# Two pacing constants of the last image's depthwise convolution are lowered, so its taps are laid out denser on VectorE

## The chip, the cores and the metric

The kernel runs on one core of a Trainium2 chip. The metric is the device time of one execution in microseconds. All arithmetic is float32. The engines are named as in the profile: PE is TensorE, DVE is VectorE, ACT is ScalarE, POOL is GpSimd, SP is SyncE, which issues most DMAs.

## The reference

The input is x, 8 images of 384 channels by 32 by 32. Two layers follow one another.

Layer 0 is a transformer block over the 1024 pixels of an image: layernorm, q, k and v, eight heads of attention, a projection with a residual, layernorm, and an MLP with a residual.

```python
xn = layernorm(xf, g1, beta1)
qkv = jnp.einsum('bnc,oc->bno', xn, w_qkv) + b_qkv
...
x1 = out + shortcut
xn2 = layernorm(x1, g2, beta2)
h = jax.nn.gelu(jnp.einsum('bnc,oc->bno', xn2, w_fc1) + b_fc1, approximate=False)
y = x1 + jnp.einsum('bnh,oh->bno', h, w_fc2) + b_fc2
```

Layer 1 takes that result and computes a depthwise convolution of 7 by 7, a layernorm over channels, w1 with GELU, a global response normalization (GRN), and w2 with a residual.

```python
y = jax.lax.conv_general_dilated(x, dw_w, padding=((3, 3), (3, 3)), feature_group_count=DIM, ...)
y = (y - mu) * jax.lax.rsqrt(var + EPS) * ln_w + ln_b
y = jax.nn.gelu(jnp.einsum('bhwc,cd->bhwd', y, w1) + b1, approximate=False)
gx = jnp.sqrt(jnp.sum(jnp.square(y), axis=(1, 2), keepdims=True))
nx = gx / (jnp.mean(gx, axis=-1, keepdims=True) + GRN_EPS)
y = grn_gamma * (y * nx) + grn_beta + y
return identity + (jnp.einsum('bhwd,dc->bhwc', y, w2) + b2)
```

## The kernel before

**Layout and stages.** Channels lie on the 128 partitions in three tiles (ct = 0, 1, 2), pixels along the free axis, in halves of 512. An iteration of the loop in `main` (L1543) does the attention and the MLP of image b and the second layer of image b-1. The depthwise convolution is no matrix product: it is 49 multiply-adds (taps) per channel tile on DVE (`convolution`, L972; L996 for the first tap, L998 for the others), spread beside PE's products. The convolution of image b runs on DVE while PE works on w1 and w2 of image b-1 and on the attention and the MLP of image b+1.

**The last image.** Image 7 has no later image beside which its convolution could run. So its MLP is done by halves of the pixels (`mlp_by_halves`, L928): fc1 and fc2 of half 0, then of half 1. A convolution row needs three rows on either side, so rows 0 to 12 can be convolved once half 0 is through, and rows 13 to 31 after half 1. As each of fc2's three output tiles is done, DVE adds it to the residual (`add_first`, L794), ACT copies it into the padded image (`pad_half`, L790), and `last_convolution` (L1530) is called. On the first tile of each half it starts a convolution: 147 taps (3 x 49) over 13 rows, then 147 over 19 rows. The second is hung behind the first.

Three layernorms follow in the same way, over the rows in `LAST` (L1138): norm a (rows 0 to 12, 416 pixels) is hung behind the first convolution, norm b (rows 13 to 21, 288 pixels) behind the second, norm c (rows 22 to 31, 320 pixels) behind norm b. Each is a chain over four engines (`layernorm`, L399): two adds on DVE (L413, L416), a sum over channels as a product with ones on PE (ln_sum, L380), the subtraction of the mean on DVE (L423), squares on ACT (L430), two adds on DVE (L434, L437), a second sum on PE (ln_var, L380), logarithm and exponential on ACT (L447, L448), and the scaling on DVE (L451).

PE meanwhile does, in this order: fc2 of half 0, fc1 and fc2 of half 1 (L351), w1 of image 6 (`grn_up_straight`, L1091, products at L338), w1 of image 7 for rows 0 to 12 (`last_up`, L1160, products at L1168, tiles h_last; it needs norm a), five of the six blocks of w2 of image 6 (`grn_down_straight`, L1104, products at L1124, added to the residual on DVE at L1132), w1 of image 7 for rows 13 to 21 (needs norm b) and for rows 22 to 31 (needs norm c), the last block of w2 of image 6, and w2 of image 7. Image 6's own layernorm (a chain of the same lines, with its channel sums folded by two DMAs on POOL, L388 and L394) runs during fc2 of half 0 and fc1 of half 1. The GRN scale of image 6 (`grn_scale`, L1176) starts as the first h_last tiles do: a product over gx (gxsum, L1182), a chain of small DVE operations (L1185 to L1190), and the scaling of w2's first tiles on DVE (L1210) and ACT (L1207).

**What sets the order.** All engines run programs that are written in one pass; each engine executes its own in order. `Flow` (L112) keeps a clock, `now`, that counts the planned length of PE's products (0.857 us for one of 512 columns, L67). A chain is a Python generator that yields how long to wait until its next step. After every product, the chains that are due write their next instructions. A chain started with `paced=True` counts its waits from when the last step was due, the others from when it was written. `finish` writes all that is left of a chain at once. `after` (L1230) lets a chain begin when another one has been written to its end, asking every 1.0 us.

In `convolution` the mean planned distance of two taps is `us`; each tap's own share of it goes by its size (L980). So 147 taps take 147 x `us` of planned time, whatever DVE needs for them. A step that is written early is not executed early unless its engine is free; it stands ahead of what is written after it.

**Buffers around it.** PSUM has four single banks, tag "o" (fc1, fc2, norm sums, gxsum, h_last, w2), and two pairs, tag "s" (w1 of image 6). A bank is given again when its last reader is done. Weights are held in a ring of nine tiles (`Weights`, L254), loaded by SP in the order of use. SP also stores the image (`keep`, L953), which waits for the last L794.

Of the kernel before, what the change touches and what calls it, by code (L numbers as in the profile page):

```python
# [151 lines left out]
def block_kernel(  # L152
# [71 lines left out]
    def col(name, i):  # L224
        at, width = VEC[name]
        assert i < width
        return vec[:, at + i : at + i + 1]

    def inner(ct):
        return pad[:, ct, PAD : PAD + H, PAD : PAD + W]  # L230

    def image(ap):
        return ap.rearrange("p (h w) -> p h w", h=H)
# [729 lines left out]
    def inside(dy, dx, y0, y1):  # L963

        rows = slice(max(y0, PAD - dy), min(y1, H + PAD - dy))
        return rows, slice(max(0, PAD - dx), min(W, W + PAD - dx))

    def size(dy, dx, y0, y1):
        rows, cols = inside(dy, dx, y0, y1)
        return 120 + (rows.stop - rows.start) * (cols.stop - cols.start)  # L970

    def convolution(acc, us, first=(), y0=0, y1=H, ready=tuple(range(CT)), taken=None):  # L972

        done = [0] * CT
        ct, n = None, 0
        taps = KS * KS - (HELPED if taken is not None else 0)

        shares = [size(*divmod(i, KS), y0, y1) for i in TAPS[:taps]]  # L980
        shares = [taps * s / sum(shares) for s in shares]
        while min(done) < taps:
            left = [c for c in ready if done[c] < taps and not (taken and taken.get(c, 0) > flow.now)]
            if not left:
                yield 1.0
                continue
            ct = min([c for c in left if c != ct] or left, key=lambda c: done[c])
            i = done[ct]
            share = shares[i]
            dy, dx = divmod(TAPS[i], KS)  # L990
            rows, cols = inside(dy, dx, y0, y1)
            window = inner(ct)[:, rows.start + dy - PAD : rows.stop + dy - PAD, cols.start + dx - PAD : cols.stop + dx - PAD]
            dst = image(acc[:, ct, :])[:, rows, cols]
            tap = col("dww", ct * KS * KS + TAPS[i])
            if i == 0:
                nc.vector.tensor_scalar(dst, window, tap, col("dwb", ct), ALU.mult, ALU.add)  # L996
            else:
                nc.vector.scalar_tensor_tensor(dst, window, tap, dst, ALU.mult, ALU.add)  # L998
            done[ct] += 1
            n += 1  # L1000
            yield share * next((early for m, early in first if n <= m), us)
# [228 lines left out]
    def after(first, chain, us=0):  # L1230
        if us:
            yield us
        while first is not None and first.gi_frame is not None:
            yield 1.0
        yield from chain
# [202 lines left out]
    def main():  # L1438
# [52 lines left out]
        def conv_norm(b, ln):  # L1491

            if b > 0:
                acc = state["acc"]
                how = dict(wait=5.0) if b < B - 1 else dict(wait=3.4, factor=2.4)
                norm = abreast(acc, acc, eps1, "lnw", f"ln3_{b - 1}", True, **how)
                if b < B - 1:
                    norm = sequence(norm, block_differences(acc))
                state["norm3"] = flow.spawn(after(ln, after(state["help"], after(state["conv"], norm))))

        def next_norms(b):

            if b > 0:
                flow.finish(state["help"])
                flow.finish(state["conv"])
            if b + 1 < B:
                xn = state["xn"] = load_x(b + 1, "xn")
                name = f"ln1_{b + 1}"
                places = (lambda: weight_places(name)) if b else averages
                norm = abreast(xn, xn, eps0, "g1", name, True, places=places, gentle=b > 0, factor=1.4 if b else 1.7)  # L1510
                state["norm1"] = flow.spawn(after(state["norm3"], norm, 50 if b else 11))
# [11 lines left out]
        last = wqkv[:, : CT * N].rearrange("p (c n) -> p c n", c=CT)  # L1523

        def last_norm(part, slow):
            return layernorm(last, last, part, eps1, "lnw", f"ln3_{B - 1}", True, slow=slow)

        ready = [], []

        def last_convolution(h, ct, ln=None):  # L1530
            if ct < 0:
                conv_norm(B - 1, ln)
                next_norms(B - 1)
                return
            ready[h].append(ct)
            if ct == 0:
                rows = (LAST[0].stop // W, H) if h else (0, LAST[0].stop // W)
                conv = convolution(last, 0.86 if h else 0.66, (), *rows, ready[h])
                state["conv"] = flow.spawn(after(state["conv"], conv), paced=True)
                if h == 0:  # L1540
                    state["norm_a"] = flow.spawn(after(state["conv"], last_norm(LAST[0], 2.6)))

        for b in range(B):  # L1543
# [6 lines left out]
            if b < B - 1:  # L1550
                mlp(b, xt, xn, weights, b, ln2, rest, lambda: next_norms(b), lambda ln: conv_norm(b, ln))
            else:
                acc = state["acc"]
                mlp_by_halves(b, xt, xn, weights, ln2, rest, last_convolution)
# [184 lines left out]
```

## Time and profile before

| what | us |
|---|---|
| median of six runs | 3304.83 (3301.5 to 3305.07) |
| the profiled execution, its own time | 3301.38 |
| its span | 3299.6 |
| PE busy | 3269.9 (99%) |
| DVE busy | 2396.8 (73%) |
| first convolution on DVE (first and last start of the stretch) | 2947.8 to 3040.3 |
| second convolution on DVE | 3040.3 to 3167.4 |
| norm a: ln_sum and ln_var on PE | 3050.62 and 3066.77 |
| gxsum of image 6 on PE; L1190 on DVE | 3098.49; 3099.57 |
| norm b: from L413 to the first h_last behind it | 3169.07 to 3176.21 |
| w2 of image 6, first five blocks on PE | 3116.86 to 3168.38 |

Lines of the profile give an engine, a line of the kernel, the operation, the tiles (written <- read), shapes, a count, busy time, and the idle time before with what ended it. A float32 product counts as two records on PE. The granted clock is 1.00 when TensorE runs at full speed. The waits view has the engine and line that waited, what it waited for, the total, the times, and the longest.

### The profile page before, as it was taken

What the parts mean: (1) busy time and instruction counts of PE and PEld (TensorE: products, weight loads), DVE (VectorE), ACT (ScalarE), POOL (GpSimd) and SP (SyncE); (2) the same over time, 40 slices, a digit from 0 to 9 for tenths busy, and PEclk for the clock granted to TensorE, in tenths of its full rate; (3) what the DMA queues carried; (4) which work ended last, traced back from release to release, by engine and by line L of the source; (5) the groups of instructions that cost most, each with busy time, mean ns of one, the idle gap of its engine ahead of it and who ended that gap; (6) DMA issues with size and microseconds to landing.
All of it is one profiled execution on the core that took longest, in us unless ns stands there. A gap on an engine that the chain in (4) does not pass through costs nothing.

```text
span 3299.6 us, 38767 instructions
## 1 busy us (share of the span) xinstructions
PE 3269.9 (99%) x14296; PEld 1408.2 (43%) x14296; DVE 2396.8 (73%) x3186; ACT 1605.5 (49%) x2194; POOL 484.3 (15%) x569
## 2 busy tenths in 40 slices
PE   8999999999999999999999999999999999999998
PEld 4344434443344433444344443444434444344455
DVE  4445787887857978579786797767876788879840
ACT  2542663446634375353662636526474355623541
POOL 2121210112110121101211021110221112100000
PEclk9999999999999999999999999999999999999999
DMA  5336732657245563537436374273842647333231
GB/s 198 112 108 147 151 67 69 159 116 151 56 99 140 137 126 57 130 109 167 92 58 144 103 184 76 53 167 90 186 72 60 179 90 173 70 78 90 68 97 43
DMA packets 199109, 368.73 MB, mean 112 GB/s; under 512 B 40768, under 2 KB 46784, under 8 KB 198528
## 3 DMA queue, kind: packets, MB, share of 16 engines
q0 software_dynamic: 80896, 158.63, 26.3%
q1 hardware_dynamic: 117728, 206.83, 20.8%
q8 instruction: 115, 1.88, 0.2%
q10 hardware_dynamic: 288, 0.71, 0.1%
q14 instruction: 82, 0.67, 0.1%
HBM read 187.03 MB, written 34.60 MB: 67 GB/s over the span
## 4 chain that ended last, share of the span: by engine, by line
PE 89%; DMA 0%; issue 0%; DVE 0%; POOL 0%; ACT 0%; POOLq 0%; DVEq 0%
PE fc L351 15%; PE s L664 11%; PE o L684 11%; PE h L358 10%; PE fc_p L358 10%; PE o_p L358 9%; PE qk L358 6%; PE o L1124 4%; PE proj L606 3%; PE v L592 3%; PE h_last L1168 2%; PE h L338 2%; PE ln_var L394 1%; PE ln_sum L394 0%; PE ln_var L380 0%
## 5 line engine op out<-in xcount | busy, mean ns | idle before, releaser
L998 DVE SCALAR_TENSOR_TENSOR acc<-pad,vec,acc 128x870 f32<-128x870 f32 (+7 forms) x861 | 963.9, 1156 | 9.0 <-DMA acc<-tap 4.3
L673 ACT ACTIVATE p<-s 128x1024 f32<-128x1024 f32 x512 | 524.3, 1024 | 282.8 <-PE s L664 275.7
L664 PE MATMUL s<-qk 48*64 48x512 f32 x4096 | 546.7, 592 | 0.2 <-ACT qk L505 0.2
L684 PE MATMUL o<-p,v 64*64 64x512 f32 x4096 | 543.2, 589 | 0.0
L351 PE MATMUL fc<-xn,fc 128*128 128x512 f32 x1152 | 502.3, 594 | 0.0
L1020 POOL DMA_DIRECT2D acc<-tap x294 | 253.5, 876 | 1209.1 <-ACT tap L1019 776.4
L351 PEld LDWEIGHTS fc<-xn,fc 128*128 128x128 f32 x1152 | 217.5, 190 | 280.6 <-issue 269.0
L358 PE MATMUL fc_p<-hid,fc 128*128 128x512 f32 x728 | 317.7, 593 | 0.0
L370 ACT ACTIVATE hid<-fc,bfc_f 128x512 f32<-128x512 f32 x192 | 131.3, 686 | 344.0 <-PE fc L351 343.8
L684 PEld LDWEIGHTS o<-p,v 64*64 64x64 f32 x4096 | 163.3, 133 | 280.7 <-issue 272.3
L664 PEld LDWEIGHTS s<-qk 48*64 48x64 f32 x4096 | 159.7, 133 | 279.2 <-issue 223.2
L358 PE MATMUL o_p<-y,w 128*128 128x512 f32 x624 | 270.9, 592 | 0.0
L1069 DVE TENSOR_TENSOR y<-h,y 128x512 f32<-128x512 f32 x288 | 197.0, 690 | 89.8 <-PE h L358 75.2
L1019 ACT ACTIVATE tap<-pad,vec 128x512 f32<-128x512 f32 x294 | 213.0, 734 | 19.5 <-DMA acc<-tap 19.4
L358 PEld LDWEIGHTS fc_p<-hid,fc 128*128 128x128 f32 x728 | 137.7, 190 | 176.4 <-issue 172.4
L358 PE MATMUL h<-acc,w_A 128*128 128x512 f32 x432 | 207.3, 595 | 0.0
L358 PEld LDWEIGHTS o_p<-y,w 128*128 128x128 f32 x624 | 118.0, 190 | 148.7 <-issue 132.0
L998 DVE SCALAR_TENSOR_TENSOR wqkv<-pad,vec,wqkv 128x377 f32<-128x377 f32 (+24 forms) x288 | 177.4, 694 | 0.6
L625 DVE TENSOR_TENSOR attn<-o,attn 128x512 f32<-128x512 f32 x64 | 44.2, 690 | 166.6 <-ACT attn L623 166.6
L790 ACT COPY pad<-x 128x512 f32<-128x512 f32 x48 | 30.2, 635 | 248.4 <-DVE x L856 192.5
L549 DVE TENSOR_TENSOR qk<-qk,qk 128x512 f32<-128x512 f32 x168 | 114.5, 689 | 37.2 <-PE qk L358 28.2
L592 PE MATMUL v<-wqkv,xn 128*128 128x384 f32 x384 | 127.7, 490 | 0.0
(311 smaller groups left out, 3750.7 us busy)
## 6 DMA issues: line engine op xcount, KB each, us to landing
acc<-tap POOLq DMA_DIRECT2D x294, 256.0 KB, 3.5
w_A<-in_w SPq DMA_DIRECT2D x72, 384.0 KB
fc<-s_fc SPq DMA_DIRECT2D x91, 256.0 KB
hid<-hid POOLq DMA_DIRECT2D x42, 512.0 KB, 7.1
fc<-in_wfc SPq DMA_DIRECT2D x54, 384.0 KB
w<-s_w SPq DMA_DIRECT2D x78, 256.0 KB
y<-y POOLq DMA_DIRECT2D x36, 512.0 KB, 7.0
kept<-x SPq DMA_DIRECT2D x8, 1536.0 KB
```

Source lines behind the costliest of these rows:

```text
L351: nc.tensor.matmul(out=ps, lhsT=lhsT(k), rhs=rhs(k)[:, half(h)], start=(k == 0), stop=(k == nk - 1))
L358: nc.tensor.matmul(out=bank, lhsT=lhsT, rhs=rhs, start=k == 0, stop=k == len(pairs) - 1)
L370: nc.scalar.activation(dst, src, function, **kw)
L592: nc.tensor.matmul(out=ps[:, :C], lhsT=xn[:, k, t * P : (t + 1) * P], rhs=wv_sb[:, k, :], start=(k == 0), stop=(k == CT - 1),)
L664: nc.tensor.matmul(out=s[64 * i : 64 * i + 64, j, :], lhsT=kT[64 * j : 64 * j + HD, m, k0 : k0 + 64], rhs=qT[64 * j : 64 * j + HD, m, half ...
L673: nc.scalar.activation(p, s, AF.Exp)
L684: nc.tensor.matmul(out=outs[i][64 * j : 64 * j + 64, :], lhsT=v[keys, t, at : at + 64], rhs=p[keys, j, :], start=(t == 0), stop=(t == KT - 1),
L998: nc.vector.scalar_tensor_tensor(dst, window, tap, dst, ALU.mult, ALU.add)
L1019: nc.scalar.mul(t.rearrange("p (h w) -> p h w", w=W), window, tap)
L1020: nc.gpsimd.dma_start(out=acc[:, ct, half(h)], in_=t, accum_op=ALU.add)
L1069: nc.vector.tensor_tensor(dst, bank, part, ALU.add)
L1124: nc.tensor.matmul(out=ps, lhsT=tiles[k], rhs=y(k, part), start=(k == 0), stop=(k == HT - 1))
```

## The change

The two paces of the last image's convolution are lowered: from 0.66 to 0.56 us per tap for the first 13 rows, and from 0.86 to 0.72 for the other 19. The taps, their order among themselves and all other instructions are the same. In the written order, 147 taps take 82.3 us of planned time instead of 97.0, and then 105.8 instead of 126.4. What is hung behind a convolution is written earlier by as much, and more taps stand ahead of what is written at a fixed point beside them.

```diff
             if ct == 0:
                 rows = (LAST[0].stop // W, H) if h else (0, LAST[0].stop // W)
-                conv = convolution(last, 0.86 if h else 0.66, (), *rows, ready[h])
+                conv = convolution(last, 0.72 if h else 0.56, (), *rows, ready[h])
                 state["conv"] = flow.spawn(after(state["conv"], conv), paced=True)
                 if h == 0:
                     state["norm_a"] = flow.spawn(after(state["conv"], last_norm(LAST[0], 2.6)))
```

## The prediction

> **What bounds the kernel now.** Read first: the busy shares and the chain that ended last. TensorE is busy for 99% of the span, and the chain runs on it.
>
> ```profile
> span 3299.6 us, 38767 instructions
> PE 3269.9 (99%) x14296; PEld 1408.2 (43%) x14296; DVE 2396.8 (73%) x3186; ACT 1605.5 (49%) x2194; POOL 484.3 (15%) x569
> PE 89%; DMA 0%; issue 0%; DVE 0%; POOL 0%; ACT 0%; POOLq 0%; DVEq 0%
> ```
>
> So time is gained or lost only where TensorE waits. Second: the waits of TensorE between 2940 and 3180 us, the stretch in which the last image's convolution lies.
>
> ```profile
> PE ln_var L380 <- DVE ln_sq L437: 2.4, 1, 2.4
> PE ln_sum L380 <- DVE ln_a L416: 1.7, 1, 1.7
> PE h_last L1168 <- DVE wqkv L451: 1.6, 1, 1.6
> ```
>
> All three belong to the second layernorm (rows 13 to 21, "norm b"), which starts only when the convolution is through, after 3168 us. They sum to 5.7 us. Behind them the clock is lower, by the windows (length, PE, PEld, DVE, ACT, POOL, granted clock, DMA):
>
> ```profile
> 3172.00:3174.00 2.00, 0.74 (x2) 0.50 (x2) 0.96 (x3) 1.80 (x3) 0.00 (x0) 0.56 0.00 1
> 3176.00:3178.00 2.00, 1.79 (x4) 1.36 (x5) 1.91 (x5) 0.90 (x1) 0.00 (x0) 0.50 0.00 0
> 3180.00:3184.00 4.00, 4.00 (x18) 3.11 (x17) 1.29 (x3) 2.62 (x9) 0.00 (x0) 1.00 0.34 98
> ```
>
> Third: what VectorE has free in the same stretch.
>
> ```profile
> 2947.00:3041.00 94.00, 91.26 (x170) 1.00 0.34 93
> 3041.00:3095.00 54.00, 52.15 (x75) 1.00 0.14 38
> 3099.00:3168.00 69.00, 60.58 (x91) 1.00 0.32 92
> ```
>
> This view carries the forecast: over the first convolution (2947 to 3041) VectorE is busy 91.26 of 94 us. Fourth: the timeline of VectorE, for the places where another engine needs it (start, length, line, operation).
>
> ```profile
> 2977.81 0.69 DVE L437 TENSOR_TENSOR attn<-attn 128x512 f32<-128x512 f32 x1
> 3029.60 0.75 DVE L794 SCALAR_TENSOR_TENSOR x<-fc,vec,x 128x512 f32<-128x512 f32 x1
> 3042.59 0.59 DVE L416 TENSOR_TENSOR ln_a<-ln_a,wqkv 128x416 f32<-128x416 f32 x1
> 3060.76 0.59 DVE L437 TENSOR_TENSOR ln_sq<-ln_sq,ln_sq 128x416 f32<-128x416 f32 x1
> 3075.26 18.88 DVE L998 SCALAR_TENSOR_TENSOR wqkv<-pad,vec,wqkv 128x551 f32<-128x551 f32 x26
> 3098.65 0.17 DVE L1185 TENSOR_REDUCE gmean<-gxsum 128x1 f32<-128x12 f32 x1 [4.51 <-PE gxsum L1182]
> 3099.57 0.17 DVE L1190 TENSOR_SCALAR gscale<-gscale 128x12 f32<-128x12 f32 x1
> 3100.66 22.82 DVE L998 SCALAR_TENSOR_TENSOR wqkv<-pad,vec,wqkv 128x589 f32<-128x589 f32 x33
> ```
>
> And the chain, for when TensorE comes to norm a's two sums:
>
> ```profile
> 3050.62 0.70 PE ln_sum L380 x2
> ...
> 3066.77 0.70 PE ln_var L380 x2
> ```
>
> TensorE came to norm a's sum 7.4 us after L416 was done (3043.2) and to its variance 5.4 us after L437 (3061.35): two margins that the pacing leaves.
>
> **The change, part by part.** No instruction is added or removed. The pace decides between which products a tap is written, and each engine keeps its written order. TensorE's own work is unchanged, so I measure positions by the time at which TensorE reached them in this trace.
>
> *The first 147 taps* begin behind w2 of the MLP's first tile, at 2943.3 (2964.89, where fc1's second half begins, less two tiles of 10.3 and the 1.0 of sums between). At 0.66 they take 97.0 us of written order, at 0.56 82.3: they end 14.7 us earlier, with rounding to grn_up's steps 15.4. Everything hung behind them moves with them: norm a's sum from 3050.62 to 3035.2, its variance from 3066.77 to 3051.4. VectorE can't follow, for it had 2.1 us of gaps there (three waits of 0.70 for a padded copy, which stay). Its work up to L416 is that of before less the third L794, now written behind: 3043.2 - 0.7 = 3042.5, less up to 1 for a shorter queue at the start; I take 3042.0. TensorE waits 6.9 us by then. Two waits on the way are inside this 6.9, not added: the last image's fc1 needs the bank that L794 of the third tile empties, six taps later (6 x 0.53 = 3.2 us, no margin seen in the trace); and the variance of image 6's layernorm needs L437 at 2977.81, seven taps (3.7 us) later, against a margin of 1.7.
>
> *Norm a's variance.* From L416 to L437 VectorE has 24 taps instead of 20 (counted by laying the taps out with the code's own rule): 24 x 0.72 (the row of 26 in 18.88) = 17.3, then L423 1.6, L434 and L437 1.2, the postponed L794 0.7 and a wait of 0.7 for its padded copy: 21.5, so 3063.5. TensorE would come at 3042.1 + 16.15 = 3058.3 and waits 5.2 more; it is now 12.1 late.
>
> *GRN's scale of image 6.* The chain L1185 to L1190 stays where it is written, but 100 taps of the second convolution stand before it instead of 65 (57.7 us of written order at 0.86 against 72.3 at 0.72; the trace's rows give the 65). From L437: 74 taps x 0.71 (between the rows of 26 and of 33) = 52.5, L451 1.75, the chain 1.1: L1190 ends at 3118.9 instead of 3099.74. VectorE's gap of 4.51 us before L1185 is filled, but not enough. Queued on ScalarE behind L1190 are six scalings (L1207, 1.85 us) and then the GELU and square of the fourth h_last tile, which free its bank: in the trace 3.4 us from L1190 to that bank, so 3122.3. With four banks the eighth h_last tile needs it; TensorE began that tile at 3091.5 + 7 x 2.09 + 0.12 = 3106.3. It is 16.0 us late. This contains the 12.1, since each wait ends at a time that VectorE sets.
>
> *Norm b and norm c.* The second convolution is through on VectorE at about 3118.9 + 1.0 (L1210) + 47 taps x 0.68 + one L1132 of 0.7 = 3152.6, L416 at 3153.5; norm b's sum is written at 3137.2, plus 16.0 = 3153.2. Its wait is 0 to 1 us, its other steps lie beside w2's products, which last until 3168.4 + 16.0, and norm c follows there. Saved: 5.7 us of waits, and the half clock behind them. The 16 records from 3176.21 take 5.55 us, at the later rate (28 in 6.79) 3.88: 1.7 us. Together 7.4.
>
> *The clock after the new waits.* The row that is nearest is the one just used: three waits within 8 us, then 1.7 us lost. The last two waits (at the seventh and eighth h_last tile, together about 4 us) can bring 0 to 1.7; I take 0.8. What is lost behind the earlier waits ends in the next wait. The Trainium skill, page "TensorE: Matmul & The Clock Gate", section "Why this matters for your kernels", says that no idle gap should exceed about 3 us, or the array falls back to half rate. By it norm b's gaps, the longest 2.44, should not have done so, and the trace shows 0.50 behind them; the waits of 5 to 7 us at norm a should, at some 1.7 us each, which speaks against the change, and counted in full the sum would be 3.4 us higher.
>
> *Queues passed.* SP's store of the image (L956) waits for the third L794, which ends at 3043 instead of 3030; weight loads queue behind it, but nine tiles are held ahead, and those asked for behind the store are first used after 3091: nothing. ScalarE's third pad copy (L790) waits for the same L794 with the first GELUs of grn_up behind it: two PSUM pairs cover it, and TensorE stands at norm a's sum meanwhile. POOL's two sums for image 6's norm wait for L437 as counted. Other DMAs keep their place.
>
> *Sum.* +16.0 - 7.4 + 0.8 = +9.4 us. The profiled execution has 3301.38 (span 3299.6 and 1.8 around it), so 3310.8; the median of the six runs, 3304.83, lies 3.45 above it, so I forecast 3314.2, slower by 0.28%. A measurement here can tell about 0.2% (6.6 us) from no change. Own range: VectorE's taps 2% quicker or slower move L1190 by 3, the clock 0 to 1.7, norm b's wait 0 to 1: 3311.4 to 3319.
>
> **The rivals.** *VectorE keeps up (faster).* If norm a's sum and variance and GRN's scale are met without waiting, only the 7.4 us remain: 3297.4. For it: 13 us of gaps after 3060. Against it: 2.1 us of gaps before 3041, where 15 are asked. It decides if TensorE's lateness at the eighth h_last tile stays under 0.8 us; the working has 16.
>
> *Waits at norm a alone.* If the four banks and ScalarE's queue hide the later scale, lateness stays at 12.1: 12.1 - 7.4 = +4.7, 3309.5, inside what counts as the same. It needs L1190 before about 3115, six taps fewer than counted.
>
> *Nothing is hidden in return.* If norm b's sum waits too and its steps slip behind w2, +16.0 without the 7.4: 3320.8. For it: margin at norm b's sum is nil. Against it: VectorE has no tap left after L416, and 30 us of w2 remain.
>
> **How the numbers follow.** Forecast 0.62 (nine tenths of it above 3311.4), waits at norm a alone 0.22, nothing hidden 0.10, VectorE keeps up 0.06. Slower: 0.56 + 0.10, and a little of the second, 0.69; faster 0.05; same 0.26. The range takes in the forecast and most of the second: 3305.5 to 3320.
>
> **What would show it.** Right: waits of some 7 and 5 us at L380 behind L416 and L437 before 3065; L1190 near 3119; a short wait of h_last on ScalarE or VectorE; no gap at L1132's last rows; norm b beside L1124. Wrong: no wait at L380 (VectorE had room), or L1190 under 3110.

## The result, and the profile after

The changed kernel takes 3311.78 us (median of 16 runs, 3310.44 to 3314.85), the kernel before 3303.67 (median of 36 runs, 3301.39 to 3306.8; the six runs shown before the prediction had 3304.83). The ratio is 1.0025 with an interval of 1.0018 to 1.0031: slower by 8.1 us. The profiled execution of the changed kernel took 3310.92 us, with a span of 3309.1.

The page of the changed kernel: busy shares, and by engine the chain that ended last.

```profile
span 3309.1 us, 38766 instructions
PE 3273.0 (99%) x14296; PEld 1409.4 (43%) x14296; DVE 2396.5 (72%) x3186; ACT 1603.4 (48%) x2192; POOL 483.9 (15%) x569
DVE 7%; PE 4%; DMA 0%; issue 0%; ACT 0%; DVEq 0%
```

TensorE is still busy for 99%, but up to 3155 us the chain no longer runs on it. The chain is followed only as far back as 2927 us, so its shares are small; what matters is where it changes engine. These are pieces of it in order of time (start, length, engine, tile, line):

```profile
2983.80 20.92 DVE wqkv L998 x42
...
3081.95 37.86 DVE wqkv L998 x54
3120.85 0.96 DVE w_A L1210
3121.80 24.24 DVE wqkv L998 x37
...
3155.43 0.72 PE ln_sum L380 x2
3156.15 6.87 PE o L1124 x16
```

Read it backwards from the last line: w2's products (L1124) came behind norm b's sum on TensorE, that sum came behind VectorE's last taps and the two adds that follow them, and from there the chain is one queue of taps back to 2984 and beyond. VectorE sets the pace through the whole stretch, up to norm b's sum. In the kernel before, TensorE did.

The waits of TensorE between 2940 and 3200 us (who, for whom, total, times, longest):

```profile
PE ln_sum L380 <- DVE ln_a L416: 4.5, 2, 4.3
PE ln_var L380 <- DVE ln_sq L437: 3.4, 1, 3.4
PE fc L351 <- DVE acc L423: 2.1, 1, 2.1
PE h_last L1168 <- ACT h_last L1173: 1.4, 1, 1.4
PE fc L351 <- DVE x L794: 1.0, 1, 1.0
```

Five places now wait where norm b alone did; norm b's variance and the h_last behind norm b have left the list, and norm b's sum adds 0.16. The timeline of TensorE shows where (start, length, line, shapes, records, idle time before):

```profile
2971.07 5.39 PE L351 MATMUL fc<-xn,fc 128*128 128x512 f32 x12 [2.10 <-DVE acc L423]
2977.49 10.66 PE L351 MATMUL fc<-xn,fc 128*128 128x512 f32 x24 [1.03 <-DVE x L794]
3044.30 1.32 PE L380 MATMUL ln_sum<-ln_a,ones 128*128 128x416 f32 x2 [4.30 <-DVE ln_a L416]
3065.83 1.75 PE L380 MATMUL ln_var<-ln_sq,ones 128*128 128x416 f32 x2 [3.42 <-DVE ln_sq L437]
3123.93 10.74 PE L1168 MATMUL h_last<-wqkv,w_A 128*128 128x416 f32 x30 [1.36 <-ACT h_last L1173]
3155.43 0.72 PE L380 MATMUL ln_sum<-ln_a,ones 128*128 128x288 f32 x2 [0.16 <-DVE ln_a L416]
3162.85 0.65 PE L380 MATMUL ln_var<-ln_sq,ones 128*128 128x288 f32 x2
```

The sum of norm a comes at 3044.30 instead of 3050.62: the denser pace did write it earlier, and TensorE stood 4.30 us before it. The sums of norm b (3155.43, 3162.85) lie beside w2. And the timeline of VectorE, for the operations that end those waits:

```profile
3043.66 0.59 DVE L416 TENSOR_TENSOR ln_a<-ln_a,wqkv 128x416 f32<-128x416 f32 x1
3065.19 0.59 DVE L437 TENSOR_TENSOR ln_sq<-ln_sq,ln_sq 128x416 f32<-128x416 f32 x1
3081.86 37.94 DVE L998 SCALAR_TENSOR_TENSOR wqkv<-pad,vec,wqkv 128x589 f32<-128x589 f32 x54
3119.71 0.17 DVE L1185 TENSOR_REDUCE gmean<-gxsum 128x1 f32<-128x12 f32 x1
3120.64 0.17 DVE L1190 TENSOR_SCALAR gscale<-gscale 128x12 f32<-128x12 f32 x1
3154.82 0.46 DVE L416 TENSOR_TENSOR ln_a<-ln_a,wqkv 128x288 f32<-128x288 f32 x1
```

54 taps run without a break up to L1185: the gap of 4.51 us that stood there is full, and the last step of GRN's scale (L1190) starts at 3120.64 instead of 3099.57.

Two profiled executions can be some microseconds apart before the stretch begins. A mark that no edit here touches, the channel sum of image 6's layernorm (L394), starts at 2957.76 before and at 2959.10 after. The 1.34 us between them are taken off below where a position of after is set against one of before; the same is done for the experiments.

### The profile page after: what moved, and what is told of

Same layout as the page of the kernel before. It is cut to its first block, busy times and chain, and to the rows that moved or that the text cites. A ratio compares the mean times of both kernels' runs of the same rounds, so it can differ in the third digit from the quotient of the medians.

```text
span 3309.1 us, 38766 instructions
## 1 busy us (share of the span) xinstructions
PE 3273.0 (99%) x14296; PEld 1409.4 (43%) x14296; DVE 2396.5 (72%) x3186; ACT 1603.4 (48%) x2192; POOL 483.9 (15%) x569
## 5 line engine op out<-in xcount | busy, mean ns | idle before, releaser
L998 DVE SCALAR_TENSOR_TENSOR wqkv<-pad,vec,wqkv 128x290 f32<-128x290 f32 (+21 forms) x288 | 177.4, 699 | 0.7
```

## The experiments

Theory: the pace only says what is written, VectorE works at its own rate, and each needed result comes as late as the taps that stand before it in VectorE's queue. Rivals: the new waits come from where norm a is asked for, or a denser pace costs time wherever it is used. Some of the runs start from the kernel before, some from the changed one; the diffs show which.

### The first pace alone

```diff
-                conv = convolution(last, 0.86 if h else 0.66, (), *rows, ready[h])
+                conv = convolution(last, 0.86 if h else 0.56, (), *rows, ready[h])
```

> First pace 0.56, second left at 0.86. Theory (VectorE's backlog sets when TensorE may go on; each wait ends at a time that VectorE sets): the waits on the way to norm a's variance stay (together some 11 us, norm a's sum about 4, its variance about 3), but only about 84 taps of the second convolution stand before L1190, so it ends near 3109 and the eighth h_last tile doesn't wait. Norm b lies partly beside w2. In sum 2 to 5 us over before: 3305.5 to 3309. Rival (the loss lies in norm a's waits, and the second pace only brings the gain of norm b): norm b stays uncovered, so the loss comes without the gain, 13 us or more over before: 3316.

Measured: 3308.01 us (3306.32 to 3310.01) beside 3304.15, ratio 1.0011 (1.0002 to 1.0021). The timeline in this kernel, of TensorE at norm a and of VectorE at GRN's scale:

```profile
3045.55 1.75 PE L380 MATMUL ln_sum<-ln_a,ones 128*128 128x416 f32 x2 [3.46 <-DVE ln_a L416]
3065.03 0.97 PE L380 MATMUL ln_var<-ln_sq,ones 128*128 128x416 f32 x2 [0.35 <-DVE ln_sq L437]
...
3112.62 0.17 DVE L1185 TENSOR_REDUCE gmean<-gxsum 128x1 f32<-128x12 f32 x1 [2.19 <-PE gxsum L1182]
3113.55 0.17 DVE L1190 TENSOR_SCALAR gscale<-gscale 128x12 f32<-128x12 f32 x1
```

VectorE waits 2.19 us for TensorE there, so it has caught up: the waits of 3.5 at norm a's sum and of 3.1 at fc1 cost their time, and the queue ahead of GRN's scale does not. The wait at norm a's variance, expected near 3 us, is only 0.35. From the sum's start TensorE itself took 19.1 us to that wait, where 16.15 were needed before, and the granted clock is 0.50 from 3046 to 3050. Of norm b's three waits the one behind L451 is left (1.3), as the second pace is the old one. Alone, this constant slows by 3.9 us.

### The second pace alone

```diff
-                conv = convolution(last, 0.86 if h else 0.66, (), *rows, ready[h])
+                conv = convolution(last, 0.72 if h else 0.66, (), *rows, ready[h])
```

> First pace left at 0.66, second 0.72. Theory: norm a is asked for when VectorE has it, no wait at L380 before 3070; about 78 taps before L1190 fill VectorE's gaps of 2.1 and 4.5 us, so it ends near 3103 and costs under 1 us at the h_last tiles; norm b goes beside w2 and gives back its waits and the half clock, together 8.7 us by the changed kernel's trace. So 7 to 9 us under before: 3295 to 3297. Rival (any denser layout of the second convolution piles up in front of the GRN scale, as more taps stand before it): L1190 some 9 us later, most of it on TensorE, and the time within 2 us of before.

Measured: 3297.22 us (3296.7 to 3298.38) beside 3304.15, ratio 0.9979 (0.997 to 0.9988). The waits of TensorE in the stretch, all of them:

```profile
PE ln_sum L380 <- DVE ln_a L416: 0.9, 1, 0.9
PE h_last L1168 <- ACT h_last L1173: 0.4, 1, 0.4
```

This half of the change is a gain: norm b lies beside w2 with a wait of 0.9 at its sum, and nothing waits for long before it. L1190 ends at 3103.7 (3105.60 less this run's 1.9), 4 us later than before, which the four banks cover but for 0.4. So a denser pace is not bad as such. The two halves, +3.9 and -6.9 apart, give +8.1 together: they don't add, since the taps that the first makes late and the taps that the second adds stand in one queue.

### Norm a asked for 15.4 us later

```diff
                 conv = convolution(last, 0.72 if h else 0.56, (), *rows, ready[h])
...
-                    state["norm_a"] = flow.spawn(after(state["conv"], last_norm(LAST[0], 2.6)))
+                    state["norm_a"] = flow.spawn(after(state["conv"], after(None, last_norm(LAST[0], 2.6), 15.4)))
```

> Both paces as changed, but norm a is written 15.4 us later, where it stood before. Theory: the two waits at L380 (4.3 and 3.4 us) get smaller or turn into waits for ScalarE's queue, L1190 stays near 3120, since the same taps stand before it, and the eighth h_last tile waits until the same moment: the time stays within 2 us of the changed kernel (3310 to 3313.5), the waits only move. Rival (the two waits at norm a are the price): they go, and with them 7 to 10 us: 3302 to 3305.

Measured: 3311.08 us (3308.71 to 3312.41) beside 3304.15, ratio 1.0019 (1.001 to 1.0028). The waits of TensorE:

```profile
PE h L338 <- ACT h L1100: 3.9, 1, 3.9
PE ln_var L380 <- DVE ln_sq L437: 3.5, 1, 3.5
PE fc L351 <- DVE acc L423: 2.1, 1, 2.1
PE h_last L1168 <- ACT h_last L1173: 1.3, 1, 1.3
PE fc L351 <- DVE x L794: 1.0, 1, 1.0
```

The sum of norm a waits no more, and nothing is gained: the wait of 4.3 became one of 3.9 in w1 of image 6. There the GELU's second pass (L1100) stands on ScalarE behind the third pad copy, and that waits for the last L794, which stands on VectorE behind the taps. GRN's scale ends at the same place (3119.4). So where norm a is asked for was not the cause. Whether the taps ahead are, the next run shows.

### Fewer first taps

```diff
                 conv = convolution(last, 0.72 if h else 0.56, (), *rows, ready[h])
...
             if i == 0:
                 nc.vector.tensor_scalar(dst, window, tap, col("dwb", ct), ALU.mult, ALU.add)
+            elif y1 == LAST[0].stop // W and i % 5 == 0:
+                pass
             else:
```

> Both paces as changed, but every fifth tap of the first 147 is left out on VectorE (27 taps, some 14 us of work), with its place in the written order kept as time; the convolution's values are therefore not the reference's in rows 0 to 12. Theory (VectorE lacks about 15 us there): VectorE keeps up, no wait at L380 before 3070, L1190 near 3105, at most 2 us lost at h_last, norm b beside w2: 5 to 8 us under before, 3296 to 3299. Rival (the early written order itself, or transfers and ScalarE, cause the waits): they stay, and the time stays over 3308.

Measured: 3298.12 us (3295.8 to 3300.28) beside 3304.15, ratio 0.998 (0.9971 to 0.9989). Both paces are those of the change, and this kernel leaves out 27 of the first convolution's 147 taps, every fifth of those that only add; at 0.53 us each that is 14 us of VectorE's work. The waits of TensorE (the lines stand two further down in this kernel):

```profile
PE h_last L1170 <- ACT h_last L1175: 1.6, 1, 1.6
PE h_last L1170 <- DVE gmean L1187: 0.6, 1, 0.6
PE ln_sum L380 <- DVE ln_a L416: 0.2, 1, 0.2
```

The written order is that of the change and the waits at fc1 and norm a are gone (the 0.2 lies at norm b's sum). GRN's scale, whose last step is L1192 here, is through at 3105.6 on the time scale of before, 14 us earlier than in the changed kernel. So the order by itself costs little: the 2.2 us at h_last. What costs is that it asks VectorE for some 14 us more than it can do by then.

### The second pace between

```diff
-                conv = convolution(last, 0.86 if h else 0.66, (), *rows, ready[h])
+                conv = convolution(last, 0.74 if h else 0.66, (), *rows, ready[h])
```

> First pace 0.66, second 0.74. Theory: some two taps fewer than at 0.72 stand before L1190, it ends near 3102 and no h_last tile waits; norm b is written 2 us later and VectorE is ready for it; no wait of TensorE is left in the stretch. 8.5 us under before and 0.5 to 1.5 under second pace 0.72: 3294.5 to 3297. Rival (the gain grows with the density of the second pace): 1 to 2 us over second pace 0.72, about 3298.5.

Measured: 3294.91 us (3292.97 to 3295.81) beside 3303.44, ratio 0.9974 (0.9964 to 0.9984). TensorE has no wait at all between 2940 and 3200 us. The timeline of TensorE, at norm b:

```profile
3158.22 0.65 PE L380 MATMUL ln_sum<-ln_a,ones 128*128 128x288 f32 x2
3171.20 3.56 PE L1168 MATMUL h_last<-wqkv,w_A 128*128 128x288 f32 x14
```

Norm b's sum lies beside w2, and the first h_last behind it starts without idle time. This is the best version found; it beats both kernels. Against 0.72 it gains 8.5 us for 6.9, each beside its own runs of before; the intervals of the two ratios overlap, and in the traces it lacks the waits of 0.9 and 0.4.

### A second pace beyond VectorE's rate

```diff
-                conv = convolution(last, 0.86 if h else 0.66, (), *rows, ready[h])
+                conv = convolution(last, 0.64 if h else 0.66, (), *rows, ready[h])
```

> First pace 0.66, second 0.64, closer than VectorE's 0.70 us per tap. Theory (taps written closer than VectorE takes them pile up in front of whatever TensorE needs next): nothing at norm a (under 0.5 us), but L1190 ends near 3110, TensorE waits 6 to 8 us at the seventh and eighth h_last tile and 4 to 5 us for norm b's sum: 2 to 5 us over before, 3305 to 3309, in spite of norm b lying beside w2. Rival (only the first pace harms, the denser second one only brings norm b's gain): 3295 to 3298.

Measured: 3308.62 us (3306.91 to 3312.04) beside 3303.44, ratio 1.0016 (1.0007 to 1.0025). The timeline of TensorE at GRN's scale and at norm b's sum:

```profile
3111.47 14.73 PE L1168 MATMUL h_last<-wqkv,w_A 128*128 128x416 f32 x36 [5.17 <-DVE gmean L1185]
...
3154.84 0.75 PE L380 MATMUL ln_sum<-ln_a,ones 128*128 128x288 f32 x2 [4.60 <-DVE ln_a L416]
```

The slowing of the first constant appears with the second alone, once its pace (0.64 per tap) lies below the 0.68 to 0.72 that VectorE takes for one: waits of 5.2 at GRN's scale (6 to 8 was expected) and of 4.6 at norm b's sum, none at norm a. So it is no matter of which convolution is pressed: for the second, 0.86 gives 3303, 0.74 gives 3295, 0.72 gives 3297, 0.64 gives 3309.

A tap's own length is not the whole rate. In the first convolution a tap takes 0.53 us, less than the pace of 0.56. But 78 us for its 147 taps are only part of the 91.26 us for which VectorE was busy there before; the rest is other work between the taps, and at 0.56 the order leaves 82.3 us. In the second, VectorE is busy for 110.7 of the 112 us from 3045 to 3157 already at 0.74. A denser pace hardly ends the convolution sooner: norm b's L416, which follows its last taps, ends at 3154.1 (0.74), 3154.4 (0.72), 3152.8 (0.64) and 3153.9 (both lowered), all on the time scale of before, where it ended at 3170.0.

### The array kept busy through norm b

The kernel before, with seven products of 384 columns that nobody reads put into norm b's waits.

```diff
-        flow.finish(norm_b)
...
+        for step, _ in enumerate(norm_b):
+            extra = {0: 2, 1: 3, 5: 2}.get(step, 0)
+            if extra:
+                bank = o_tile(f"warm_{step}")
+                for _ in range(extra):
+                    nc.tensor.matmul(out=bank[:, :C], lhsT=ident, rhs=wproj_sb[:, 0, :], start=True, stop=True)
```

> The kernel before with seven products of 384 columns that nothing reads, written into norm b's three waits (two, three and two; 0.64 us each at full clock, 4.5 us of the 5.7). Theory (norm b costs 8.7 us in the kernel before: 5.7 of waits and 2.8 because the idle array falls to half clock, under which norm b's variance and the first h_last tiles run): the granted clock stays at 1.00 from 3168 to 3182, the waits themselves stay, and the time falls by 2 to 3 us. Rival (the clock falls for another reason, or what went with the waits was not the clock): the clock still falls, or the time stays or rises by up to 1 us.

Measured: 3301.11 us (3298.39 to 3303.18) beside 3303.44, ratio 0.9993 (0.9984 to 1.0002): by time alone this can't be told from no change. In windows of this kernel (bounds, length, busy time of PE, PEld, DVE, ACT and POOL, granted clock, DMA):

```profile
3172.00:3174.00 2.00, 2.00 (x7) 1.36 (x8) 1.19 (x3) 0.72 (x2) 0.00 (x0) 1.00 0.73 268
3176.00:3178.00 2.00, 1.67 (x6) 0.68 (x5) 1.00 (x3) 1.95 (x3) 0.00 (x0) 1.00 0.00 0
```

The clock stays at 1.00 where it was 0.56 and 0.50, and the 16 records of h_last behind norm b's variance take 4.15 us instead of 5.55. From the end of w2's five blocks to the start of its last one the kernel needs 45.65 us (3170.14 to 3215.79) instead of 47.62. So some 2.0 us of norm b's cost before were the half clock; what is left of it was waiting.

## Why the prediction was right, step by step

The predicted 3314.2 us stands against 3311.78, near the lower end of the narrower range, and the sum of +9.4 against +8.1 between the medians (+8.2 between the spans, with the 1.34 taken off). Half of the 2.4 us between forecast and result is before's own median, 1.16 lower in the later runs than in the six shown.

*Norm a's sum.* 6.9 late was said, with L416 done at 3042.0; TensorE's sum came at 3042.96 (3044.30 less 1.34), 7.8 late. The lateness was right, its place was not: 3.13 of it were met at fc1. The step had allowed for waits on the way, but not for these: it named the bank that L794 empties with 3.2 us, which cost 1.03, and the variance of image 6's norm, which cost nothing. The 2.10 behind L423, the subtraction of the mean in image 6's norm, it did not name.

*Norm a's variance.* 12.1 late was said and 13.1 measured (3064.5 for 3063.5). The wait before it is 3.42 instead of 5.2, because TensorE was slow on the way: the same 36 products' records and the two of the sum that took 16.15 us before took 18.11. The windows of the changed kernel (columns as above) show why:

```profile
3046.00:3048.00 2.00, 2.00 (x4) 0.69 (x3) 1.69 (x3) 1.97 (x3) 0.00 (x0) 0.50 0.74 299
...
3066.00:3068.00 2.00, 2.00 (x3) 1.00 (x4) 2.00 (x4) 0.38 (x1) 0.00 (x0) 0.50 0.01 4
...
3120.00:3124.00 4.00, 2.64 (x9) 1.17 (x7) 3.79 (x9) 3.12 (x10) 0.00 (x0) 1.00 0.34 98
```

Behind each of the two waits the granted clock is 0.50. What TensorE loses there it doesn't wait later: the half clock is hidden in the lateness that VectorE sets, as the step on the clock said.

*GRN's scale.* 16.0 late at the eighth h_last tile was said, from 100 taps that stand before L1185; it is 16.3 (3122.6 for 3122.3), with L1190's end at 3119.5 for 3118.9. This carried the forecast and it held: counting the taps and giving each its row's time was worth more than any statement on shares.

*The saving, the term that was mis-sized.* 7.4 was said and 8.2 measured. Pieces of the chain, two of the kernel before and then two of the changed one:

```profile
3189.62 26.38 PE h_last L1168 x100
3216.00 6.87 PE o L1124 x16
...
3188.61 36.84 PE h_last L1168 x144
3225.45 6.87 PE o L1124 x16
```

From the end of w2's five blocks to the start of its last block TensorE took 47.62 us before and takes 36.84 now. The norm sums that lay in between now lie beside w2, and make the way from the eighth h_last tile to the end of the five blocks 2.55 longer (64.68 for 62.13). 47.62 - 36.84 - 2.55 is 8.2. Of it 5.7 are the waits, as said. The h_last products took 38.72 (5.55 + 6.79 + 26.38) and take 36.84: 1.9, where 1.7 was taken. The four norm sums took 3.2 and take 2.3: 0.9, which the step had not counted; norm b's variance alone took 1.34 at half clock, and 0.75 in the run that kept the array busy. Of the other side 0.16 is the wait at norm b's sum, and 0.1 isn't assigned. (The 8.7 in two expectations has the sums at their planned length, 2.04, and no wait.)

*The clock after the new waits.* 0.8 was said, 0 to 1.7 possible; it is 0. The wait at h_last is 1.36 instead of about 4, since 1.5 us of the lateness went into the half clock behind norm a's variance (41.68 us from there to h_last, where 92 records at full rate and the sum make 40.2), and behind 1.36 the window above shows 1.00. With these two terms the sum is +16.3 - 8.2 = +8.1, and the stretch as a whole shows the same: the last block of w2 starts at 3225.45, less 1.34, against 3216.00.

The Trainium skill, page "TensorE: Matmul & The Clock Gate", section "Why this matters for your kernels", sets the bound for an idle gap at about 3 us. The single gaps agree: 4.30 and 3.42 were followed by 0.50, as was the 3.46 of the first pace alone, and 1.36 by 1.00. The gaps of 1.70, 2.44 and 1.62 us of norm b, within 7.8 us, don't: behind them the clock was 0.50 as well, and filling them kept it at 1.00. Here a series of short gaps, 5.7 us idle out of 7.8, did what a single long one does.

*The rivals.* The time of "VectorE keeps up", 3297.4, is nearly that of the second pace alone, 3297.22, where VectorE does keep up but for 1.3 us of waits; with both paces lowered its condition, under 0.8 us late at the eighth h_last tile, was missed by 15. "Waits at norm a alone" needed L1190 before 3115; it came at 3119.5. "Nothing is hidden in return" came to 0.16 us of wait at norm b's sum: the margin was nil, as said. The working could not tell 0 from 1 us there, so that it came out so small is partly luck.

*Queues.* No cost of SP's later store or of POOL's sums shows in any wait. ScalarE's pad copies wait 69.4 us in all instead of 55.9, which costs nothing in the changed kernel and 3.9 us where norm a was asked for later: the named cover, TensorE's own stand at norm a, was gone there.

Not settled is why the mark before the stretch moves by up to 4 us between profiled executions of kernels that do the same until there.

## What to carry to other kernels

A pace in a written program is a claim on a rate. Once the engine is busy throughout, the other work between the steps included, a denser pace finishes hardly anything earlier, and it puts the surplus ahead of everything that is written later on that engine: here the surplus, gone when 14 us of taps were left out, came back as waits at five places, and moving one of them only moved its wait. So count the steps that stand before each needed result, by their own durations, in the stage in question (91 of 94 us busy here, 73% over the span), and make the pace denser only where the engine has gaps: lowering the second constant alone to 0.74, close above VectorE's 0.68 to 0.72, gained 8.5 us, and lowering both lost 8.1.

## What the runs showed of the hardware

- Three gaps of 1.70, 2.44 and 1.62 us within 7.8 us brought the granted clock to 0.50; gaps of 2.10 and 1.03 with 5.4 us of products between them left the clock at 1.00 in the windows from 2971 to 2990, and 1.36 alone left it there too.
- A single gap of 4.30 or 3.42 us cost 2.0 and 1.5 us more in products at half clock behind it, and the 3.46 of the first pace alone cost 3.0 (19.1 us for 16.15): the price does not follow the length of the gap. Behind the 5.17 of the run at 0.64, 36 records took 14.6 us up to the next product's start (3111.47 to 3126.04), where by the rate of the same products before (52 in 18.26) they need 12.6.
- Seven products of no use, put into the gaps, held the clock at 1.00 and took 2.0 us out of the stretch, though over the whole kernel the interval reaches to no change.
